# Score buffers with fixed places, and the long product of heads 0 and 1 moved to second place

## The chip, the core and the metric

The kernel runs on one core of a Trainium2 chip. A core has a matrix engine (TensorE, "PE" in the profile), a vector engine (DVE), a scalar engine (ACT), a general engine (POOL) and DMA queues; SP issues most DMAs. [...] The metric is the device time of the core in microseconds (us). Before the change it is 1812.58 us, the median of three runs (1812.48 to 1813.05).

## The reference

The input is an image batch of 32 x 256 x 32 x 32. Every image is normalised in groups of channels, projected to queries, keys and values with 8 heads of 32 channels, put through attention over its 1024 places, where a place sees only places before it, and added back to the input.

```
x = x + conv(group_norm(x))
q = q_w @ x + q_b;   k, v = split(kv_w @ x + kv_b)
scores = q . k / sqrt(32), where(key < query), else -10000
attn = where(key < query, softmax(scores), 0)
out = attn @ v
```

Everything is fp32.

## The kernel before, in words

**Tiling.** Images are taken one after the other. Of each, four heads at a time (a group `g` of two) are worked on, and the 1024 x 1024 scores of a group, of which only about half are needed, are cut into six visits (`VISITS`, line 557). So an image has N = 12 visits, and the kernel 384. Visits are numbered 0 to 383 here, and the kind of a visit is its number modulo 6.

**A visit's score phase** (`scores`, line 339). Scores are computed transposed: keys on the partitions, queries along the free axis. A head has only 32 channels, so a product uses 32 rows of the matrix array, and 64 of its columns, for 64 keys. Eight such small products, four heads by two halves of the keys, fit side by side in the array. Head j always uses row group j. A visit fills three pairs of PSUM banks: `pairs[0]` takes the long products of heads 0 and 1, `pairs[1]` those of heads 2 and 3, and `pairs[2]` the short products of all four, where heads 0 and 2 share one bank and heads 1 and 3 the other. Below, L01 and L23 are the long products of heads 0, 1 and of heads 2, 3, and S01 and S23 are the short ones. In program order a phase of kinds 1, 3 and 5 is:

- S23: four products of 128 columns, then four of 64 columns
- L01: four of 512 columns
- L23: four of 512 columns
- a wait for the semaphore `bank_free` (line 366), which each of the four last products of S23 raises by one
- S01: four of 128 columns, then four of 64

Two row groups write to one bank in S23 and in S01, and the wait keeps them apart in time. Kind 0 is alike, but has its long products in two pieces (128 and 384 columns). In kinds 2 and 4 the short products are one piece of 256 columns (they aren't in `PAIRS`, line 566), and kind 4 has the long ones in two pieces.

**After the products** ACT takes the exponentials, in the order `pairs[0]`, `pairs[1]` (line 384), `pairs[2]` (`eh`, line 380). POOL masks the diagonal blocks out of `eh` (line 330), and DVE adds exponentials over keys (line 427).

**The order of work.** It is written out by hand: instructions are issued per engine in program order (line 630). The loop at line 705 issues, for step i, the score phase of visit i, then the work that `when(...)` put there (projections of a coming image, line 162, among others), then the products of exponentials and values of visit i - 1 (`values`, line 399, instructions at line 409). So the matrix engine changes from 32-row to 128-row products after each score phase and back before the next. In the last image the projections run out, and the last six visits follow each other more closely.

**Score buffers.** All three pairs come from one pool of three buffers with one tag, "sT" (lines 119 and 347). A new pair takes the buffer that came free first. In the built program that makes `pairs[2]` of a visit the successor of `pairs[0]` of the visit before, `pairs[0]` the successor of `pairs[1]`, and `pairs[1]` that of `pairs[2]`. So S23 waits for the first of the three exponentials of the visit before, L01 for the second, and L23 for the third. A wait that an earlier one covers isn't issued.

## Time and profile before

The profile shows one execution. "Span" is the time from the first to the last instruction of the core.

| what | value |
|---|---|
| median of the runs | 1812.58 us |
| the profiled execution, its own time | 1813.86 us |
| span of the profiled execution | 1812.2 us |
| PE busy | 1797.5 us (99%) |
| DVE busy | 1643.0 us (91%) |
| ACT busy | 1457.2 us (80%) |
| POOL busy | 919.4 us (51%) |
| granted TensorE clock | 0.999 |
| share of score products (L302) in the chain that ended last | 30% |

A fp32 product stands in the trace as two weight loads and two matmuls, since it goes through the array in two passes. Matmuls overlap, so their busy times in a group add up to more than the time they take together. Besides durations, the trace records when each semaphore was raised.

### The profile page before, as it was taken

The numbers are of one execution on the slowest core, as the hardware profiler recorded it, in microseconds if no ns is written. First come the engines' busy times: TensorE is split into PE (matmuls) and PEld (weight loads), VectorE is DVE, ScalarE is ACT, GpSimd is POOL, SyncE is SP. The second block draws the span as 40 slices with busy tenths as digits, with TensorE's granted clock in tenths as the row PEclk, the third lists the DMA queues.
The fourth block names the chain that finished last, engine by engine and source line by source line (L and its number), as shares of the span: only waits on it lengthen the run. The fifth ranks groups of instructions, "written<-read, shape, count | busy, mean of one in ns | idle before, by whom it ended". The sixth has DMA issues, their size and how long they took to land.

```text
span 1812.2 us, 81732 instructions
## 1 busy us (share of the span) xinstructions
PE 1797.5 (99%) x37036; PEld 956.9 (53%) x37036; DVE 1643.0 (91%) x1832; ACT 1457.2 (80%) x1985; POOL 919.4 (51%) x901
## 2 busy tenths in 40 slices
PE   9999999999999999999999999999999999999997
PEld 5555555555555555555555555555555555555553
DVE  4689999999999999999999999999999999999987
ACT  6888878888778888788887888887888878888774
POOL 2345555545545555455555455554554555555532
PEclk9999999999999999999999999999999999999999
DMA  3457676776766766766767667677667676675653
GB/s 124 72 96 142 130 138 124 137 149 130 147 118 137 145 131 139 133 132 133 148 135 146 111 137 153 125 142 132 136 132 147 132 140 122 134 156 121 124 113 85
DMA packets 86531, 236.78 MB, mean 131 GB/s; under 512 B 21280, under 2 KB 22304, under 8 KB 70304
## 3 DMA queue, kind: packets, MB, share of 16 engines
q0 software_dynamic: 15872, 97.53, 35.8%
q1 hardware_dynamic: 70304, 133.96, 28.2%
q8 instruction: 290, 4.75, 1.1%
q14 instruction: 65, 0.53, 0.1%
HBM read 66.85 MB, written 34.57 MB: 56 GB/s over the span
## 4 chain that ended last, share of the span: by engine, by line
PE 98%; DVE 1%; ACT 0%; issue 0%; DMA 0%; POOL 0%; DVEq 0%
PE sT L302 30%; PE acc L409 27%; PE pp L162 26%; PE ppv L162 13%; PE pd L461 0%; ACT e L384 0%; PE pv L162 0%; DMA x<-in_x_dram 0%; DVE diagonal L427 0%; DVE st L177 0%; DVE e L427 0%; PE pm L162 0%; POOL diagonal L330 0%; ACT eh L380 0%; DVE rb_last L528 0%
## 5 line engine op out<-in xcount | busy, mean ns | idle before, releaser
L330 POOL TENSOR_SCALAR_AFFINE_SELECT diagonal<-eh 128x512 f32<-128x512 f32 x512 | 649.1, 1291 | 748.6 <-ACT eh L380 748.4
L384 ACT ACTIVATE e<-sT 128x1024 f32<-128x1024 f32 x768 | 745.2, 1022 | 260.7 <-PE sT L302 256.7
L302 PE MATMUL sT<-q,k 32*64 32x128 f32 (+2 forms) x18432 | 584.9, 372 | 0.5 <-issue 0.3
L427 DVE TENSOR_TENSOR e<-e,e 128x1024 f32<-128x1024 f32 x315 | 553.6, 1757 | 21.6 <-ACT v L266 4.8
L302 PEld LDWEIGHTS sT<-q,k 32*64 32x64 f32 x18432 | 405.4, 131 | 181.4 <-PE sT L302 59.3
L162 PE MATMUL pp<-xn,wT 128*32 128x512 f32 x4096 | 493.3, 598 | 0.6 <-issue 0.3
L409 PE MATMUL acc<-e,v 128*32 128x384 f32 (+3 forms) x4608 | 401.8, 450 | 0.0
L380 ACT ACTIVATE eh<-sT 128x768 f32<-128x768 f32 (+1 forms) x384 | 340.9, 888 | 0.0
L409 PEld LDWEIGHTS acc<-e,v 128*32 128x32 f32 x4608 | 149.7, 110 | 261.0 <-issue 238.0
L162 PE MATMUL ppv<-wT,xn 128*32 128x256 f32 x4096 | 247.5, 382 | 0.0
L162 PEld LDWEIGHTS pp<-xn,wT 128*32 128x32 f32 x4096 | 107.8, 109 | 200.1 <-issue 165.9
L427 DVE TENSOR_TENSOR diagonal<-diagonal,e 128x1536 f32<-128x1536 f32 x126 | 188.4, 1495 | 16.8 <-PE acc L409 9.1
L427 DVE TENSOR_TENSOR e<-e,eh 128x1024 f32<-128x1024 f32 x127 | 176.0, 1386 | 6.9 <-DVE e L427 0.5
L427 DVE TENSOR_TENSOR e<-e,diagonal 128x2048 f32<-128x2048 f32 x62 | 142.1, 2293 | 39.2 <-POOL diagonal L330 36.2
L409 PEld LDWEIGHTS acc<-diagonal,v 128*32 128x32 f32 x4096 | 119.6, 110 | 92.9 <-issue 75.7
L162 PEld LDWEIGHTS ppv<-wT,xn 128*32 128x32 f32 x4096 | 120.4, 109 | 79.6 <-issue 7.2
L409 PE MATMUL acc<-diagonal,v 128*32 128x128 f32 x4096 | 160.4, 273 | 0.0
L235 ACT ACTIVATE xn<-x,shift,rstd 128x256 f32<-128x256 f32 x248 | 137.1, 613 | 0.0
L440 POOL DMA_DIRECT2D e<-e x124 | 102.3, 825 | 38.1 <-PE pp L162 31.1
L528 DVE SCALAR_TENSOR_TENSOR rb<-num,v_bias_col,x 128x256 f32<-128x256 f32 x248 | 117.5, 514 | 4.4
L440 POOL DMA_DIRECT2D diagonal<-diagonal x124 | 119.4, 963 | 0.0
L526 DVE TENSOR_TENSOR num<-num,rb 128x512 f32<-128x512 f32 x124 | 110.8, 894 | 0.0
(78 smaller groups left out, 1004.4 us busy)
## 6 DMA issues: line engine op xcount, KB each, us to landing
diagonal<-diagonal POOLq DMA_DIRECT2D x62, 512.0 KB, 8.3
e<-e POOLq DMA_DIRECT2D x62, 512.0 KB, 5.2
rb<-inverses SPq DMA_DIRECT2D x124, 256.0 KB, 4.7
out_dram<-rb SPq DMA_DIRECT2D x124, 256.0 KB, 5.1
x<-in_x_dram SPq DMA_DIRECT2D x120, 256.0 KB, 6.2
diagonal<-diagonal POOLq DMA_DIRECT2D x62, 256.0 KB, 4.9
folded<-diagonal SPq DMA_DIRECT2D x62, 256.0 KB, 4.4
e<-e POOLq DMA_DIRECT2D x62, 256.0 KB, 5.1
```

The source lines that it names most:

```text
L162: nc.tensor.matmul(out[part], lhsT=lhsT[:, part], rhs=rhs, start=start, stop=stop, skip_group_check=True)
L235: nc.scalar.activation(to, of, AF.Identity, bias=live["shift", b][:, g : g + 1], scale=rstd)
L302: return nc.tensor.matmul(bank[c : c + KEYS, cols], lhsT=live["k", b, g][rows, kb * P + c : kb * P + c + KEYS], rhs=live["q", b, g][rows, ...
L330: nc.gpsimd.affine_select(out=square[:, :, place + s * P : place + (s + 1) * P], in_=raw[:, :, (1 - s) * KEYS : (3 - s) * KEYS], pattern=[ ...
L380: exp = nc.scalar.activation(eh.rearrange("p (n bank) q -> p bank n q", n=2)[:, :, :, :narrow], short[:, :, :, :narrow], AF.Exp)
L384: nc.scalar.activation(e[:, 2 * a : 2 * a + 2, :wide], pairs[a][:, :, :wide], AF.Exp)
L409: nc.tensor.matmul(acc[HD * j : HD * (j + 1), of], lhsT=live["v", b][:, kb, h * HD : (h + 1) * HD], rhs=e[:, j, :], start=first, stop=last ...
L427: nc.vector.tensor_add(to, to, tile_of(b, g, at))
L440: nc.gpsimd.dma_start(out=total[:rows], in_=total[rows : 2 * rows], accum_op=ALU.add)
L526: nc.vector.tensor_mul(num, num, rb)
L528: nc.vector.scalar_tensor_tensor(blocks(rb, s), blocks(num, s, s == 1), v_bias_col[:, g : g + 1], blocks(xt[:, g, cols], s), ALU.add, ALU.add,
```

## The change

It has two parts.

1. The three pairs get a tag each, with one buffer per tag, so `pairs[a]` of a visit follows `pairs[a]` of the visit before. S23, the first of a phase, writes to `pairs[2]`, whose exponential is the last of the three, so one wait covers the phase. In the last six visits (from `TURNING` on, visit 378) the tags turn by one place at each visit, which gives the succession of before. The weight transposes and the warming products at the start get tags too.
2. In the kinds with split short products (0, 1, 3 and 5) the first piece of L01 is issued between the two pieces of S23, through the `between` hook of `scores_of`.

The built program has the same matrix, vector, scalar and POOL operations in the same order otherwise. On the matrix engine, 628 of the 958 waits of score products for ACT are gone, and 66 waits of score products for the matrix engine's own semaphore have come in (two in each of 33 visits, one of them an instruction of its own), each for a product of the visit before.

```diff
-        ps_s = tc.alloc_tile_pool(name="ps_s", bufs=3, space=PSUM)
+        ps_s = tc.alloc_tile_pool(name="ps_s", bufs=1, space=PSUM)
 ...
-            pt = ps_s.tile([P, 2, HALF], F32, tag="sT", name=f"wt_{n}")
+            pt = ps_s.tile([P, 2, HALF], F32, tag=f"s{n}", name=f"wt_{n}")
 ...
-            pt = ps_s.tile([P, 2, HALF], F32, tag="sT", name="busy")
+            pt = ps_s.tile([P, 2, HALF], F32, tag="s0", name="busy")
 ...
-            pairs = [ps_s.tile([P, 2, HALF], F32, tag="sT", name=f"sT_{name}_{a}") for a in range(3)]
+            if b * N + v >= TURNING:
+                live["places"] = live.get("places", 0) + 1
+            pairs = [
+                ps_s.tile([P, 2, HALF], F32, tag=f"s{(a + live.get('places', 0)) % 3}", name=f"sT_{name}_{a}")
+                for a in range(3)
+            ]
 ...
-            first = short_of((2, 3))
-            for n in range(len(longs) - 1, -1, -1):
-                long_of((0, 1), n)
+            begin = [lambda n=n: long_of((0, 1), n) for n in range(len(longs) - 1, -1, -1)]
+            first = short_of((2, 3), begin.pop(0)) if i in PAIRS else short_of((2, 3))
+            for f in begin:
+                f()
             long_of((2, 3), 0)
 ...
+        TURNING = (B - 1) * N + 6
```

## The prediction

> **What bounds the kernel now.** I read the page first: its busy times, then the chain that ended last.

> ```profile
> PE 1797.5 (99%) x37036; PEld 956.9 (53%) x37036; DVE 1643.0 (91%) x1832; ACT 1457.2 (80%) x1985; POOL 919.4 (51%) x901
> PE 98%; DVE 1%; ACT 0%; issue 0%; DMA 0%; POOL 0%; DVEq 0%
> PE sT L302 30%; PE acc L409 27%; PE pp L162 26%; PE ppv L162 13%; PE pd L461 0%; ACT e L384 0%; PE pv L162 0%; DMA x<-in_x_dram 0%; DVE diagonal L427 0%; DVE st L177 0%; DVE e L427 0%; PE pm L162 0%; POOL diagonal L330 0%; ACT eh L380 0%; DVE rb_last L528 0%
> ```

> The matrix engine is the chain. Next, the list of what it waits for:

> ```profile
> PE pc L548 <- DVE worst L546: 3.9, 1, 3.9
> PE busy L148 <- POOL ident masks.py:199: 1.7, 1, 1.7
> PE pm L162 <- DVE mv L178: 0.7, 1, 0.7
> ```

> Nothing of the steady state is in it, so a nanosecond gained or lost inside a score phase counts in full, once per phase. Then the timeline, for one phase of kind 3 and the mode change after it:

> ```profile
> 1004.25 1.47 PE L302 MATMUL sT<-q,k 32*64 32x128 f32 x48
> ...
> 1005.45 1.02 ACT L384 ACTIVATE e<-sT 128x1024 f32<-128x1024 f32 x1 [0.32 <-PE sT L302]
> ...
> 1005.65 0.42 PE L162 MATMUL ppv<-wT,xn 128*32 128x256 f32 x4
> ```

> A phase lasts 1.40 us from its first matmul to the first of the next mode. For its inside I took the single records of matmuls and of semaphore raises. Outside the first and last visits they repeat within 2 ns in nearly every phase of a kind. Kinds 1, 3 and 5, ns from the first matmul (first of four; the other three follow 6.6 ns apart):

> | product | pass 1 | pass 2 |
> |---|---|---|
> | S23, 128 columns | 0 | 160 |
> | S23, 64 | 269 | 325 |
> | L01, 512 | 54 | 534 |
> | L23, 512 | 384 | 815 |
> | S01, 128 | 963 | 1072 |
> | S01, 64 | 1181 | 1237 |

> So starts pass each other between row groups: L01 at 54 stands behind S23's 64-column product (269) in the program. Raises: `bank_free` at 556, 599, 641, 684; the matrix engine's own semaphore at 1185 (end of L01), 1467 (L23), 1626 (S01).

> [...] The ends I tested. With a matmul's recorded duration, S01's eight products would be through between 1072+268 = 1340 and 1257+217 = 1474, yet S01's raise comes at 1626. Let products retire in program order only, 16.7 ns each, 14 ns after their recorded end, and a raise cost another 26.3 ns: L23's fourth retires and raises at 835+587+45 = 1467, then 26.3 + 8 x 16.7 = 160 gives 1627. Kind 2 has four products behind L23's raise: 1563 + 26.3 + 4 x 16.7 = 1656, recorded 1656. Kind 0, four behind a raise at 1580: 1673, recorded 1673. So retirement in order, and with it the raise, is what this trace shows. [...] 42.7 ns between the `bank_free` raises is 16.7 + 26. [...]

> **Part 1, fixed buffers.**
> - Waits removed: 628. Visit 1's phase has no wait for ACT in the program before, and its matmuls start at 0, 54, 160, 269, 325, 384 like all others. A satisfied wait costs 0; so does its removal.
> - The wait kept is now for the last exponential. From its end to the start of the next phase there are 0.70, 0.79, 0.45 or more, 0.16, 1.14 and 0.59 us where that phase is of kind 0 to 5. The tightest is kind 2's `eh` before kind 3:

> ```profile
> 1753.84 1.03 ACT L380 ACTIVATE eh<-sT 128x1024 f32<-128x1024 f32 x1
> 1755.03 1.47 PE L302 MATMUL sT<-q,k 32*64 32x128 f32 x48
> ```

>   From the end of an exponential to the matmul it releases takes 53 ns, seen where phases do stall, near the end (visit 381: L01 after `e`, L23 after `eh`):

> ```profile
> 1783.90 0.21 PEld L302 LDWEIGHTS sT<-q,k 32*64 32x64 f32 x8 [0.27 <-ACT e L384]
> 1784.81 0.46 PEld L302 LDWEIGHTS sT<-q,k 32*64 32x64 f32 x24 [0.71 <-ACT eh L380]
> ```

>   So 161 - 53 = 108 ns are left, and that distance doesn't change: kind 2's phase keeps its order. Cost 0, hidden by the projection and the value products in between. If the engine needed the release before it drains from the last value product (202 ns before), up to 202 - 108 = 94 ns are lost in 64 phases: 6 us. I take 0.
> - 66 waits of the matrix engine for itself, all for products of the visit before: 0 to 33 x 0.05 = 1.6 us (0.05 from the 53 ns above); I take 0. At the start the tags change which product waits for which copy, long before: 0. From visit 378 the succession is the old one.

> **Part 2, L01 second.** In kinds 1, 3 and 5:
> - Gain: four products fewer are issued ahead of L01, which starts at 27 instead of 54, as in kind 2, where it is also second (27, 507). S01 would then end 27 ns earlier, at 1257; L23 (835 + 427 of streaming = 1262) ends last, against 1284 before: 22 ns.
> - Loss: S23's last products, which raise `bank_free`, now stand behind L01 and retire after it. L01 second retires at 1158 (kind 2's record). Then four raises, 43 each: 1201, 1244, 1287, 1330, instead of 684. Queued behind the wait are S01, then the whole next step. Raise to matmul is 44 ns (the 53 above less 9 from the exponential's end to its raise): S01 starts at 1374 instead of 963. It starts on an idle array, so as in visit 381 its passes stand at 0, 160, 269, 325 (+20 for the fourth): last matmul at 1719. The next mode comes 146 ns after the last matmul (1403 - 1257): 1865. That is 1865 - 1403 = 0.462 us later, and the gain is gone with it.
> - The wait decides from 936 - 44 = 892 ns on, when heads 0 and 1 have their rows free.
> - ACT isn't late: L01's exponential starts 27 ns earlier, and `eh` comes after two exponentials of 1.02, past S01.

> Kind 0: S23's 64-column products stand behind L01's 128-column piece alone, which retires at about 560 (207 + 268 + 14, and in order behind S23's first four); raises near 705, needed at 968. Its L23 is staggered by the issue and ends last: 0, at best -27 ns x 64 = -1.7 us.

> Count: 192 phases. Visit 379 is stalled by exponentials: L01 retires at 1406, S01 starts at 1622, next mode 2113 instead of 1995: +0.12. Visit 381: 2531 against 2624 anyway: 0. Visit 383: the end follows L01, its exponentials and the mask: taken as 0. 189 x 0.462 + 0.12 = 87.4 us. Span 1812.2 + 87.4 = 1899.6; own time 1813.86 + 87.4 = 1901.3; the median of the runs is 1.28 below that execution: 1900.0.

> **Rivals.**
> - *Raises come at each product's own end.* Then the fourth is at 684, before 892, and 22 ns x 192 = 4.2 us are gained: 1808. For it: starts do pass each other. Against it: three raise times to the nanosecond. 0.06.
> - *The late exponential costs too* (kind 3, 94 ns): 1900 + 6 = 1906; with the rival above, 1814, no change. 0.06 and 0.02.
> - *The stall is shorter or longer*: a restart at 109 instead of 160 ns and a mode change of 119 instead of 146 give 0.384 (1885); a raise that takes twice the 44 ns to start S01 gives 0.506 (1908). If S23's second piece were also held back until L01's second pass has begun (507), L23 would start at 622 and end at 1500, still hidden before S01's end at 1746; kind 4's L23, at 483 before L01's second pass at 618, speaks against the hold. 0.06 beyond 1884 or 1910.
> - The likeliest, 1900, has the remaining 0.80; its own range is 1886 to 1906.

> **Numbers.** The range 1884 to 1910 holds the likeliest and the late exponential, about 0.86. Outside are the gain, no change, and odd sizes. Within 0.2% (3.6 us, about what a measurement of this kernel tells from no change): 0.02; faster 0.06; slower 0.92.

> **What would show it.** In phases of kinds 1, 3, 5: L01 at 27; `bank_free` raised near 1201 to 1330; S01 at 1374; next mode at 1865; idle of about 0.1 us on the array before S01. Kinds 2 and 4 unchanged (1.476 and 1.481 us), kind 0 near 1.496. Score products' share of the chain rises from 30% to about 33%. I am wrong if `bank_free` is raised near 684, or if phases of kind 3 begin with a wait on `eh`.

## The result, and the profile after

The changed kernel takes 1898.20 us, the median of four runs (1897.97 to 1898.79). The kernel before, in four runs beside it, takes 1812.56 us (1812.48 to 1813.05). The ratio is 1.0472 (95% interval 1.0454 to 1.0491). The changed kernel's profiled execution has an own time of 1898.05 us, 84.2 us more than before, and a span of 1896.3 us.

The page of the changed kernel, first its busy times, then the chain that ended last:

```profile
PE 1882.0 (99%) x37036; PEld 938.9 (50%) x37036; DVE 1619.2 (85%) x1832; ACT 1473.8 (78%) x1985; POOL 688.7 (36%) x901
PE 99%; DVE 0%; ACT 0%; issue 0%; POOL 0%; POOLq 0%
PE sT L302 34%; PE acc L415 26%; PE pp L162 25%; PE ppv L162 13%; PE pd L467 1%; PE busy L148 0%; PE pv L162 0%; ACT e L390 0%; PE pm L162 0%; DVE rb_last L534 0%; ACT eh L386 0%; DVE rb_last L522 0%; DVE turned L519 0%; DVE acc L532 0%; DVE xn L233 0%
```

The matrix engine is still the chain, and only the score products' share grew, from 30% to 34%. POOL, with the same 901 instructions, is busy for 230.7 us less; that comes up below.

The list of what the matrix engine waits for, of the changed kernel:

```profile
PE pc L554 <- DVE worst L552: 3.9, 1, 3.9
PE busy L148 <- POOL ident masks.py:199: 1.7, 1, 1.7
PE pv L162 <- ACT k L249: 0.4, 1, 0.4
PE sT L302 <- issue: 0.4, 1, 0.4
```

It is as empty as before, though every second score phase now contains a stop, by my estimate of 0.1 us (L23's last matmul starts at 835 ns of the phase and, as its two matmuls stand 431 ns apart, has its columns through near 1266; S01 starts at 1372). The ends of matmuls in a profile are modelled, and L23's, recorded at 835 + 587 = 1422 ns, covers the stop. The idle time of the weight loads shows it. The row of the score products' weight loads from the page, of the kernel before:

```profile
L302 PEld LDWEIGHTS sT<-q,k 32*64 32x64 f32 x18432 | 405.4, 131 | 181.4 <-PE sT L302 59.3
```

and of the changed kernel:

```profile
L302 PEld LDWEIGHTS sT<-q,k 32*64 32x64 f32 x18432 | 385.9, 131 | 289.4 <-PE sT L302 182.5
```

Idle time that ended with a score product's own raise went from 59.3 to 182.5 us: 123 us in 192 phases, or 0.64 us in each. One such phase, in the timeline of weight loads, before:

```profile
310.07 0.54 PEld L302 LDWEIGHTS sT<-q,k 32*64 32x64 f32 x32 [0.20 <-ACT eh L380]
310.79 0.61 PEld L302 LDWEIGHTS sT<-q,k 32*64 32x64 f32 x16 [0.19 <-PE sT L302]
311.47 0.37 PEld L162 LDWEIGHTS ppv<-wT,xn 128*32 128x32 f32 x12
```

and after, with the line of its matmuls from the same stretch:

```profile
325.00 0.54 PEld L302 LDWEIGHTS sT<-q,k 32*64 32x64 f32 x32 [0.20 <-ACT eh L386]
325.00 1.93 PE L302 MATMUL sT<-q,k 32*64 32x128 f32 x48
326.37 0.42 PEld L302 LDWEIGHTS sT<-q,k 32*64 32x64 f32 x16 [0.83 <-PE sT L302]
326.86 0.37 PEld L162 LDWEIGHTS ppv<-wT,xn 128*32 128x32 f32 x12
```

S23, L01 and L23 load their weights in the same 0.54 us. S01's loads begin 1.37 us into the phase instead of 0.72, and the next mode comes at 1.86 instead of 1.40. The matmul line shows 48 matmuls (24 products, each recorded as two) without a gap.

The trace's single records of the changed kernel, kinds 1, 3 and 5, in ns from the phase's first matmul:

| record | before | predicted | after |
|---|---|---|---|
| L01, first pass | 54 | 27 | 27 |
| matrix engine's own raise for L01 | 1185 | 1158 | 1158 |
| `bank_free`, four raises | 556, 599, 641, 684 | 1201, 1244, 1287, 1330 | 1201, 1243, 1286, 1328 |
| S01, first matmul | 963 | 1374 | 1372 |
| last matmul | 1257 | 1719 | 1717 |
| first matmul of the next mode | 1403 | 1865 | 1863 |

And where the 84.2 us of the span are, from the same records:

| part of the span | before | after | difference |
|---|---|---|---|
| phases of kinds 1, 3, 5 (192) | 271.27 us | 358.75 us | +87.5 us |
| phases of kinds 0, 2, 4 (192) | 287.56 us | 288.48 us | +0.9 us |
| between phases | 1220.42 us | 1215.53 us | -4.9 us |
| before the first phase and after the last | 32.90 us | 33.59 us | +0.7 us |

### The profile page after: what moved, and what is told of

Same layout as the page of the kernel before. It is cut to its first block, busy times and chain, and to the rows that moved or that the text cites. A ratio compares the mean times of both kernels' runs of the same rounds, so it can differ in the third digit from the quotient of the medians.

```text
span 1896.3 us, 81766 instructions
## 1 busy us (share of the span) xinstructions
PE 1882.0 (99%) x37036; PEld 938.9 (50%) x37036; DVE 1619.2 (85%) x1832; ACT 1473.8 (78%) x1985; POOL 688.7 (36%) x901
## 4 chain that ended last, share of the span: by engine, by line
PE 99%; DVE 0%; ACT 0%; issue 0%; POOL 0%; POOLq 0%
PE sT L302 34%; PE acc L415 26%; PE pp L162 25%; PE ppv L162 13%; PE pd L467 1%; PE busy L148 0%; PE pv L162 0%; ACT e L390 0%; PE pm L162 0%; DVE rb_last L534 0%; ACT eh L386 0%; DVE rb_last L522 0%; DVE turned L519 0%; DVE acc L532 0%; DVE xn L233 0%
## 5 line engine op out<-in xcount | busy, mean ns | idle before, releaser
L330 POOL TENSOR_SCALAR_AFFINE_SELECT diagonal<-eh 128x512 f32<-128x512 f32 x512 | 441.5, 884 | 1037.0 <-ACT eh L386 1037.0
L302 PE MATMUL sT<-q,k 32*64 32x128 f32 (+2 forms) x18432 | 673.2, 374 | 0.9 <-issue 0.4
L433 DVE TENSOR_TENSOR e<-e,e 128x1024 f32<-128x1024 f32 x315 | 541.3, 1718 | 47.1 <-PE acc L415 30.9
L302 PEld LDWEIGHTS sT<-q,k 32*64 32x64 f32 x18432 | 385.9, 131 | 289.4 <-PE sT L302 182.5
L162 PE MATMUL pp<-xn,wT 128*32 128x512 f32 x4096 | 492.8, 598 | 0.2 <-DVE qk_bias L667 0.2
L162 PE MATMUL ppv<-wT,xn 128*32 128x256 f32 x4096 | 247.5, 382 | 0.0
L162 PEld LDWEIGHTS pp<-xn,wT 128*32 128x32 f32 x4096 | 107.3, 109 | 200.2 <-issue 185.0
L433 DVE TENSOR_TENSOR e<-e 128x512 f32<-128x512 f32 x64 | 69.8, 1090 | 116.9 <-ACT q L249 114.2
L433 DVE TENSOR_TENSOR e<-e,eh 128x1024 f32<-128x1024 f32 x127 | 161.9, 1275 | 6.9 <-ACT xn L235 0.5
L162 PEld LDWEIGHTS ppv<-wT,xn 128*32 128x32 f32 x4096 | 120.4, 109 | 79.6 <-issue 7.2
```

The costliest lines, as they stand in the source:

```text
L162: nc.tensor.matmul(out[part], lhsT=lhsT[:, part], rhs=rhs, start=start, stop=stop, skip_group_check=True)
L302: return nc.tensor.matmul(bank[c : c + KEYS, cols], lhsT=live["k", b, g][rows, kb * P + c : kb * P + c + KEYS], rhs=live["q", b, g][rows, ...
L330: nc.gpsimd.affine_select(out=square[:, :, place + s * P : place + (s + 1) * P], in_=raw[:, :, (1 - s) * KEYS : (3 - s) * KEYS], pattern=[ ...
L433: nc.vector.tensor_add(to, to, tile_of(b, g, at))
```

## Experiments

Theory: raises keep program order across row groups, so L01 ahead of S23's last products delays `bank_free`. Rival: the fixed buffers, or something else in a phase, cost the time. Each experiment is set against runs of the kernel before on the same chip (medians 1812.2 to 1813.4 us).

### The buffers alone

```diff
-            pairs = [ps_s.tile([P, 2, HALF], F32, tag="sT", name=f"sT_{name}_{a}") for a in range(3)]
+            if b * N + v >= TURNING:
+                live["places"] = live.get("places", 0) + 1
+            pairs = [
+                ps_s.tile([P, 2, HALF], F32, tag=f"s{(a + live.get('places', 0)) % 3}", name=f"sT_{name}_{a}")
+                for a in range(3)
+            ]
```

with the other tags of part 1, and the order of before.

> Part 1 alone: fixed buffers, the old order of products. Theory (the raise of bank_free retires behind L01): no part of the loss, 1812.6 us within 1.5 either way; bank_free raised at 556 to 684 ns, phases of kinds 1, 3 and 5 1.403 us long. Rival (the one wait for the last exponential, or the new waits of the matrix engine for itself, cost the time): near 1898 us, with a wait for eh at the head of the phases.

Measured: 1813.07 us (1811.1 to 1816.38, 12 runs) against 1813.18; ratio 1.0000 (0.9991 to 1.0009). Phases of kinds 1, 3 and 5 last 1.403 us, and `bank_free` is raised at 556, 599, 641 and 684 as before. The timeline of its matmuls in the phase shown above:

```profile
309.71 1.47 PE L302 MATMUL sT<-q,k 32*64 32x128 f32 x48
311.12 0.42 PE L162 MATMUL ppv<-wT,xn 128*32 128x256 f32 x4
```

Part 1 costs nothing and gains nothing: 628 waits that were always satisfied went, and the one that stayed isn't late either.

### The order alone

```diff
-            first = short_of((2, 3))
-            for n in range(len(longs) - 1, -1, -1):
-                long_of((0, 1), n)
+            begin = [lambda n=n: long_of((0, 1), n) for n in range(len(longs) - 1, -1, -1)]
+            first = short_of((2, 3), begin.pop(0)) if i in PAIRS else short_of((2, 3))
+            for f in begin:
+                f()
```

> Part 2 alone: the old pool of three buffers, L01 between the pieces of S23. Theory: the whole loss, 1898.2 us within 1.5; bank_free raised at 1201 to 1328 ns, S01 at 1372, phases of kinds 1, 3 and 5 1.863 us long. Rival (part 1 costs it): 1808 to 1813 us.

Measured: 1901.39 us (1898.2 to 1903.47, 4 runs), ratio 1.0489 (1.0471 to 1.0506). The profiled execution has 1898.2 us, `bank_free` at 1201, 1244, 1286 and 1329, and phases of 1.864 us. The weight loads of the phase around 324 us:

```profile
325.15 0.42 PEld L302 LDWEIGHTS sT<-q,k 32*64 32x64 f32 x16 [0.83 <-PE sT L302]
325.64 1.45 PEld L162 LDWEIGHTS ppv<-wT,xn 128*32 128x32 f32 x32
```

The same 0.83 us before S01 as with the whole change. The order makes the whole loss. The median lies 3 us above the expected 1898.2, outside the 1.5 us allowed for; what may move a median by so much is the subject of the last experiments.

### L01 ahead of S23 where S23 is one piece (kind 2)

Kinds 2 and 4 kept their order in the change. In kind 2 of the kernel before, L01 is put ahead of S23:

```diff
+            if i == 2:
+                long_of((0, 1), 0)
             first = short_of((2, 3))
             for n in range(len(longs) - 1, -1, -1):
-                long_of((0, 1), n)
+                if i != 2:
+                    long_of((0, 1), n)
```

> The kernel before, with one move: in kind 2, whose S23 is a single piece of 256 columns, L01 is issued ahead of S23. Nothing is interleaved. Theory: L01 retires at 1131 ns, bank_free is raised at 1174, 1216, 1259 and 1302, S01 starts at 1346 instead of 936, and the phase takes 1.86 us instead of 1.476: 0.383 x 64 = 24.5 us, 1837 us, or up to 4 us less if POOL's masks gain slack as they did in the changed kernel. Rival (interleaving the pieces of S23 with another row group costs the time, not the order of retirement): 1812 us or 1 to 2 less, since L01 starts 27 ns earlier.

Measured: 1844.81 us (1843.6 to 1845.83, 4 runs), ratio 1.0170 (1.0153 to 1.0187), where 1837 was expected. In kind 2 the raise for L01 comes at 1131, `bank_free` at 1174, 1217, 1259 and 1302, and S01 at 1345 (expected 1346). So the raises come in program order in another phase too, with another order of products. The size was missed by the last step: the next mode comes at 1936, not near 1860. S01 here is one piece of 256 columns, whose last matmul starts at 1632, and the mode change follows 304 ns after it; the expectation had 225. The weight loads of such a phase:

```profile
310.49 0.67 PEld L302 LDWEIGHTS sT<-q,k 32*64 32x64 f32 x24 [0.20 <-ACT q L249]
311.83 0.21 PEld L302 LDWEIGHTS sT<-q,k 32*64 32x64 f32 x8 [0.68 <-PE sT L302]
312.42 0.16 PEld L162 LDWEIGHTS pp<-xn,wT 128*32 128x32 f32 x8 [0.39 <-issue]
```

From S01's first load to the next mode's first matmul it is 0.59 us. Per phase that is 1936 - 1476 = 460 ns, x 64 = 29.4 us. Of the other parts of the profiled execution's 32 us, kind 0 has 7.5 us more, and the time between phases is 5.2 us less; both are taken up below.

### One raise instead of four

If the four raises stand one behind another, dropping three of them should bring the last forward by 3 x 26 ns. The 26 ns are an estimate from the kernel before. From L23's raise to S01's it takes 93 ns in kind 2 (1563 to 1656), where S01 has four products, and 159 ns in kinds 1, 3 and 5 (1467 to 1626), where it has eight: 16.5 ns for each product more. The `bank_free` raises, one product on each, stand 42.7 ns apart, 26 more. In the changed kernel:

```diff
-            ends = [made[-1] for made in first.values()]
+            ends = [made[-1] for made in first.values()][-1:]
```

> The changed kernel, but only the last product of S23 raises bank_free, and S01 waits for that one. Theory: L01's raise at 1158, then 26.3 + 4 x 16.7 = 93 ns to S23's raise at 1251; S01 at 1295 and the next mode at 1786, 77 ns earlier in 189 phases: 1883.6 us. Rival (products raise at their own end, and S01 is late for another reason, such as reloading weights after an interleaved product): S01 stays at 1372, 1898 us. Rival (a retirement takes 43 ns with or without a raise): 1898 us too.

Measured: 1898.62 us (1892.22 to 1903.61, 4 runs), ratio 1.0464 (1.0434 to 1.0494): against the expectation, no gain in the total. Inside the phase everything is as expected: the one raise at 1251 (93 ns behind L01's at 1158, with four products here too), S01 at 1295, the next mode at 1787 instead of 1863. The weight loads of the same phase:

```profile
324.25 0.54 PEld L302 LDWEIGHTS sT<-q,k 32*64 32x64 f32 x32 [0.20 <-ACT eh L386]
325.55 0.42 PEld L302 LDWEIGHTS sT<-q,k 32*64 32x64 f32 x16 [0.75 <-PE sT L302]
326.04 0.37 PEld L162 LDWEIGHTS ppv<-wT,xn 128*32 128x32 f32 x11
```

0.83 us before S01 became 0.75. But some phases, unlike the others of their kind, last up to 1.5 us longer. Summed over visits 12 to 377, what phases last beyond the median of their kind is 16.5 us here, against 2.6 us in the kernel before and 3.6 us in the changed one. I call these standstills. In this execution they take what the phases gave.

### POOL's late mark

The 4.9 us between phases are mostly one step: that after the phase of the second head group's kind 1 (visit number 7 within its image). Its median is 3288 ns before and 3154 ns after: 134 ns in each of 30-odd images. The value products there begin with POOL's masked block (`diagonal`), and the last thing POOL writes to it is a small fill (line 337), which marks the first place. What waited for that tile, and what ended POOL's and others' waits, from the tile's view; before:

```profile
L330 POOL TENSOR_SCALAR_AFFINE_SELECT diagonal<-eh x512: 624/1082/2792, 20.3 to 1799.1; 128x512 f32<-128x512 f32 x171
...
  POOL diagonal L330: 37.9, 36
  PE acc L409: 9.1, 3
  POOL diagonal L337: 5.6, 28
...
  PEld acc L409: 5.9, 29
```

after:

```profile
L330 POOL TENSOR_SCALAR_AFFINE_SELECT diagonal<-eh x512: 624/634/2682, 20.7 to 1882.6; 128x512 f32<-128x512 f32 x171
...
  POOL diagonal L330: 52.1, 34
  PE acc L415: 9.3, 3
  DVE diagonal L433: 0.5, 1
```

Before, weight loads waited 28 times for the fill, 5.6 us in all; after, never. And the masks' median fell from 1082 to 634 ns. To test whether that wait was the 4 us, the fill is moved ahead of the second mask in the kernel before, where it is still behind the mask that writes its place:

```diff
-            if j == 0:
-                nc.gpsimd.memset(square[0:1, :, 0:1], 1.0)
+                if (j, s) == (0, 0):
+                    nc.gpsimd.memset(square[0:1, :, 0:1], 1.0)
```

> The kernel before, with POOL's small fill of the first place of a diagonal (line 337) put between the two masks of visit kind 0 instead of after both. Theory (the changed kernel got 4 us back because POOL's masks were no longer late for the value products of kind 0 in the second head group, which were held up by 135 ns in 30 images of the kernel before): the first of the two diagonal products then waits for the first mask and the fill alone, the second mask ends near 2.71 us after the projections begin and is needed at 2.84, so the 135 ns go: 4 us, 1808.6 us where the kernel before takes 1812.6. Rival (those 135 ns have another cause): no change.

Measured: 1826.20 us (1821.08 to 1827.76, 5 runs), ratio 1.0069 (1.0055 to 1.0082): slower, where a gain of 4 us was expected. The wait itself is gone, as the tile's view shows:

```profile
  POOL diagonal L330: 38.7, 37
  PE acc L409: 9.1, 3
  ACT v L266: 0.5, 1
...
  PEld acc L409: 0.6, 2
```

and the step's median is 3154 ns, the same as in the changed kernel. So the fill was what held the step up. Summed over the images that step is 3.87 us shorter, as in the changed kernel. All in all, however, the time between phases is only 1.8 us less (1218.64 for 1220.42), since the step after kind 0's phase in the first head group grew by 2.1 us, and the phases, kind 0's above all, now hold 16.2 us of standstills, against 2.6 before.

### What a standstill is

Visit 192 of that kernel in the timeline, first its matmuls, then its weight loads:

```profile
912.66 1.42 PE L302 MATMUL sT<-q,k 32*64 32x128 f32 x51
915.18 0.44 PE L302 MATMUL sT<-q,k 32*64 32x128 f32 x13 [1.10 <-issue]
915.55 0.64 PE L162 MATMUL pp<-xn,wT 128*32 128x512 f32 x4
```

```profile
912.66 1.29 PEld L302 LDWEIGHTS sT<-q,k 32*64 32x64 f32 x52 [0.41 <-ACT v L266]
915.18 0.22 PEld L302 LDWEIGHTS sT<-q,k 32*64 32x64 f32 x12 [1.23 <-issue]
```

The same phase of the kernel before:

```profile
907.50 1.39 PEld L302 LDWEIGHTS sT<-q,k 32*64 32x64 f32 x64 [0.41 <-ACT v L266]
909.03 0.16 PEld L162 LDWEIGHTS pp<-xn,wT 128*32 128x32 f32 x8
```

The engine stops for 1.2 us inside S01, with nothing that it waits for ("issue"). Among the DMA queues there is one whose packets fit:

```profile
q8 instruction: 290, 4.75, 1.1%
```

If so, a program that is moved by a fraction of a packet should stall elsewhere. The one-raise kernel once more, and then shifted kernels: four of the warming products at the start (16 instructions) are replaced by tiny ones (32 x 2, four instructions each), so that all that follows comes later by a known count.

> The kernel with one raise once more. Its phases were 77 ns shorter, as expected, but the whole was not, since single phases of kinds 0, 4 and 5 stood still for 0.1 to 1.5 us, 16.5 us in all in the profiled execution against 3.5 in the changed kernel. If that standstill belongs to the kernel (its pace against the supply of instructions), it comes again: 1892 to 1904 us, the same visits. If it was chance: 1884 to 1887 us.

Measured: 1897.37 us (1889.96 to 1899.21, 5 runs), ratio 1.0475 (1.0460 to 1.0489). The standstills came again: of the 19 phases that stood still for over 0.1 us, 18 had done so in the first run of this kernel. The profiled execution was the fastest one, 1889.96 us, with 10.0 us of standstills. The sum closes: 1898.05 of the changed kernel, less (1863 - 1786) ns x 189 = 14.55, plus 10.00 - 3.56 = 6.44 of standstills, is 1889.94 us (what lies between the phases grew by 0.9 us, and the two ends shrank by 0.8). The single raise is worth its 14.6 us, and the standstills take back a part that differs between executions.

```diff
+        def small_ones(n):
+            pt = ps_s.tile([P, 2, HALF], F32, tag="sT", name="small_ones")
+            for _ in range(n):
+                nc.tensor.matmul(pt[:HD, 0, :2], lhsT=ident[:, :HD], rhs=ident[:, :2], start=True, stop=True)
 ...
-            keep_busy(16)
+            keep_busy(12)
+            small_ones(20)
```

This is 20 x 4 - 4 x 4 = 64 instructions later, in the kernel with the early fill:

> The kernel with the early fill, and 16 more products ahead of the first image (four of the warming products are replaced by 20 tiny ones), so that every later product stands 64 instructions further on in the matrix engine's packets of 256 instructions. In the kernel with the early fill the phases of kind 0 of the first head group stood still at one place, always 449 instructions after the start of the last packet that had landed: a packet's border, in the middle of the phase. Theory (the matrix engine waits for its instructions there): the border moves to a quarter of the phase, where 64 instructions more are slow products ahead of it; of the 16 us most goes, and with the 4 us of the early fill the time is 1808 to 1814 us. Rival (the standstill belongs to the phase and not to the border): 1821 to 1828 us again, in the same visits at the same product.

Measured: 1813.15 us (1810.97 to 1817.61, 13 runs), ratio 1.0002 (0.9993 to 1.0010). A shift of 64 instructions takes 13 us off the same program; standstills fell from 16.2 to 3.1 us. The same with `small_ones(36)`, 128 later:

> The same with 32 more products: the border moves by 128 instructions, to the start and the end of the kind 0 phase, which has 256. Theory: [...] standstills of about 1 us at its end[...]; 1820 to 1845 us. [...] 1808 to 1814 us. Rival (no border): 1821 to 1828 us with the standstill at the same product as without the shift.

Measured: 1818.46 us (1817.96 to 1822.4, 7 runs), ratio 1.0037 (1.0025 to 1.0048), 8.9 us of standstills. This lies between the theory's two ranges, 1808 to 1814 us and 1820 to 1845 us, which were guesses. With 12 and with 28 of them, 32 and 96 later:

> The early fill with 8 more products ahead: the packet border stands 32 instructions earlier in the kind 0 phase than without a shift, at three eighths of it. Theory: between no shift (16 us of standstill) and 16 products (3 us): 1809 to 1820 us, pauses again 449 instructions after the start of the last landed packet. A version that beats the kernel before would be at 1809.

> The early fill with 24 more products ahead: the border stands at an eighth of the kind 0 phase, after 32 of its instructions. Theory: few standstills in the first head group, as with 16, and some in the second, as with 32: 1809 to 1818 us. A version that beats the kernel before would be at 1809.

Measured: at 32 later, 1820.34 us (1814.96 to 1826.24, 8 runs), ratio 1.0037 (1.0024 to 1.0050), 15.5 us of standstills, just above the 1820 expected at most; at 96 later, 1817.75 us (1815.52 to 1819.64, 7 runs), ratio 1.0024 (1.0013 to 1.0035), 5.0 us, with a first phase that starts 2.4 us later than without the shift.

The expectations give a phase of kind 0 256 instructions. It has 128 (64 weight loads and 64 matmuls), so the fractions that they name are wrong. Counted in the traces, the borders do explain where these five kernels stand still. In visits 12 to 377, 100 phases of kind 0 have a border in their second half, and 55 of them stand still for over 0.1 us; of the 205 others, 3 do. Without a shift and at 32 later, such borders lie in the first head group, with 14.2 and 12.7 us of standstills there; at 96 and 128 later in the second, with 4.8 and 8.9 us there.

The shift of 64 in the one-raise kernel and in the kernel before:

> The changed kernel with one raise, and 16 more products ahead. Theory (its 14.6 us were eaten by waits for instructions): 1884 to 1889 us. Rival (something else that comes with the shorter phases): 1890 to 1900 us again.

> The kernel before with 16 more products ahead, nothing else. Theory: its standstills, 2.6 us in the profiled execution, go or move; 1809 to 1813 us. Rival (moving the borders by itself costs): above 1815 us.

Measured: with one raise, 1891.24 us (1884.89 to 1892.85, 5 runs), ratio 1.0423 (1.0406 to 1.0440), 6 us less than unshifted but above the 1884 to 1889 expected, with 11.1 us of standstills still, 9.1 of them in kinds 4 and 5 of the first head group. The kernel before, shifted, takes 1816.79 us (1814.48 to 1819.27, 13 runs), ratio 1.0021 (1.0012 to 1.0029), where 1809 to 1813 was expected; this is the range of the rival, that moving the borders costs something by itself. Its profiled execution (1815.43 us) has 3.2 us of standstills, 0.6 more than unshifted, so its median stays unexplained.

The time does depend on where the packet borders fall, by up to 13 us for one and the same work (1826.20 us unshifted, 1813.15 us at 64 later). All 34 pauses of over 0.56 us in the six shifted kernels lie at record 193 modulo 256 again, so they go with the border and not with a product. A border's place alone doesn't set the cost: the kernel before has its borders where the one with the early fill has them, and stands still for 2.6 us instead of 16.2. How late each packet lands, and why, these runs don't tell. No version was faster than the kernel before.

## Why the prediction was right

1900.0 us was predicted, 1898.2 measured. The mechanism and its size came as predicted: 87.4 us were forecast for the phases of kinds 1, 3 and 5, and they grew by 87.49. By the steps:

- **Part 1 at nothing.** Shown: with the buffers alone the ratio is 1.0000. The late exponential (a rival) didn't come: from the end of `eh` to a phase of kind 3 it is 161 ns as before, and in the phase shown the weight loads stand idle for the same 0.20 us ahead of it.
- **L01 raises at 1158, four raises follow in program order.** Shown by the raises, within 2 ns; by kind 2, where the same reckoning, with another order, gave the raises from 1174 to 1302; and by the single raise at 1251. The rival that raises come at each product's own end needed the fourth at 684 and is out. Starts pass each other (L01 at 27 ns starts ahead of the second pass, at 160, of S23's products that were issued before it), and only the raises keep the order. The trace shows the raises alone; that products without a raise retire in order between them is the prediction's estimate from their times. Its 16.7 ns for a product and 26.3 for a raise stand beside 16.5, or (159 - 93) / 4, and 26 to 27 (42.7 - 16.5 and 93 - 4 x 16.5) in the kernel before; its 14 ns lie there between the recorded end of S23's first 64-column product (325 + 217 = 542) and its raise (556).
- **S01 44 ns after the last raise, on an idle array, next mode 146 ns after the last matmul.** 44 (1328 to 1372) and 146 (1717 to 1863) as predicted, and S01's passes start 0, 160, 269 and 325 ns after its first matmul, as at the head of a phase; 1372 and 1863 for 1374 and 1865: +0.460 us per phase instead of +0.462.
- **The last image.** Visit 379 grew by 91 ns (1995 to 2086; predicted 118), visit 381 by 1 (predicted 0). In visit 383 the phase grew by 0.46 us, and the time from there to the last DVE instruction shrank by 0.46: 0, as taken.
- **Kinds 0, 2, 4 unchanged.** 1496, 1476 and 1481 ns, the same medians as before. Kind 0's L01 piece starts at 27 and `bank_free` is raised up to 703 (predicted near 705).

The terms that were mis-sized:

- **What lies between phases was taken as unchanged; it lost 4.9 us.** The step that failed is the reading of the list of waits: "Nothing of the steady state is in it". A wait of 134 ns for POOL's fill, in 30 images, was there before, hidden in that list because modelled matmul ends cover it, and visible in the weight loads. In the changed kernel, where POOL has 0.46 us more in half of the phases, it is gone, and the early fill shows it to be worth 134 ns a time. (On why the masks are faster: in both kernels a mask takes 0.62 to 0.64 us when DVE does nothing beside it, and up to 2.79 us before and 2.68 after beside a DVE sum. The longest masks of the kernel before have a whole sum of 2.29 us inside them. That the sums slow the masks was not shown: no run took the sums away.)
- **The offset from the profiled execution to the median.** The prediction subtracted 1.28 us, from one execution of the kernel before; in the changed kernel the median is 0.15 us above its profiled execution. That gives back 1.4 of the 3.3 us by which the span was too long, so the total owes a part of its closeness to chance. Standstills move an execution by this much: the two profiled executions of the one-raise kernel have 16.5 and 10.0 us of them.
- **The rival's gain.** From the start of a last matmul of 64, 128, 256 and 512 columns to the first matmul of the next mode it takes 146 (kinds 1, 3 and 5), 202 (value products), about 305 (kind 2) and 522 ns (`pd` in the last image). A straight line through the first and the last has 0.84 ns per column. The prediction gave L23's 512 columns 427 ns, or 0.83 each (in the trace of before, S01's first matmul, at 963, follows L01's second pass of 512 columns, at 534, after 429 ns), but S01's last 64 columns only 27 ns (1257 to 1284), or 0.42 each. At 0.84 (an estimate from that line), S01 ends last both times, and its earlier start would have been worth 27 ns, not 22, had the raises come early. It didn't enter the sum.

What stays open: why the standstills are 2.6 us in one kernel and 16 us in another. That they lie at a packet's border (79 of 84 pauses), and that a shift of the program moves them and changes their size, is shown; what makes a packet late is not.

## What to carry to other kernels

Before a product is moved ahead of others in another row group, look for the raises that now stand behind it. Here starts passed each other (L01 at 27 ns ahead of S23's second pass at 160), but the raises came in program order: with L01 ahead, S23's four came from 1201 to 1328 ns, behind L01's at 1158, instead of from 556 to 684. That delayed S01's weight loads by 0.64 us a phase, of which 0.46 us reached the end of the phase. Look for the matrix engine's waits in the rows of its weight loads, not only in its list of waits. And compare two kernels phase by phase before comparing totals: in this program of small products, standstills at packet borders added or hid up to 14 us.

## What the runs showed of the hardware that was not expected

- Over 290 packets of 16,384 bytes on the instruction queue, the kernel before has 74,151 records of the matrix engine, 256.1 per packet from the first packet to the 276th. Where small products use 128 instructions in 1.5 us, it stands still at some packets' borders: 71 of the 79 pauses counted there last 0.6 to 1.4 us, and the standstills of a kernel are 1.2 to 16.5 us in all.
- From one raise of the matrix engine to the next it takes 93 ns where four products are issued after the first, the last of them raising (1563 to 1656), and 159 ns where there are eight (1467 to 1626): 16.5 ns for each fp32 product more. Raises on four products in a row stand 42 to 43 ns apart (1201 to 1328 in the changed kernel), also where the recorded ends of these products, 542 to 562 ns (starts at 325 to 345, 217 long), lie long before.
- From the start of the last matmul of one mode to the first of the next it takes 146 ns where that last one has 64 columns, 304 where it has 256 and 522 where it has 512. With S01 in one piece of 256 columns behind L01 and `bank_free`, kind 2's phase ended at 1936 ns and not near 1860, so the width of the last product of a phase was part of the phase's price.
- A POOL mask of 128 x 512 takes 0.62 to 0.64 us while DVE does nothing, and up to 2.79 us beside a DVE sum (2.29 us long, kernel before).
